# A conditioned block's second MLP: its first product divided a second time, into 49 inner products in seven streams

## The chip, the cores and the metric

The kernel runs on one core of one Trainium2 chip. The metric is the time of one execution on the device in microseconds (us). Before the change it is 484.83 us, the median of three executions that ran from 484.69 to 485.11 us. A separate execution was profiled; all rows of the profile come from that one.

## What is computed

Input `x` is 32 sequences of 128 tokens of 512 features, all float32. Two modulated MLPs follow one another. The first acts only on masked tokens (few of them). The second, which takes most of the time, acts on all 4096 tokens:

```
m = mask[:, :, None]
... # first half, on the masked tokens
x = x + gate_msa[:, None] * ssm_out
shift_mlp, scale_mlp, gate_mlp = jnp.split(silu(t) @ ffada_w + ffada_b, 3, axis=1)
ff_norm = _layernorm(x) * (1.0 + scale_mlp[:, None]) + shift_mlp[:, None]
h = gelu(ff_norm @ ff_w1 + ff_b1, approximate=True)      # 512 -> 1024
out = x + gate_mlp[:, None] * (h @ ff_w2 + ff_b2)        # 1024 -> 512
```

## The kernel before, in words

After an opening of about 93 us (masked tokens, weights, the first pair's normalised tokens) the second MLP runs over four pairs `p` of token groups. A pair is 8 sequences, 1024 tokens: side 0 and side 1, with 512 tokens each. Each of the two matrix products of a pair is done by a scheme of the Strassen-Winograd kind: tokens, features and outputs are halved, and seven inner products P1 to P7 of sums and differences of blocks take the place of eight.

*First product* (`first_product`, line 687). The sums of token blocks come from `combine_x` (L655 to L665: four VectorE subtractions and additions of 128x1024), those of the weights from `combine_weights` (L286, once). Output features are taken 128 at a time: four units `u`, two at a time ("U" and "V"), each with two PSUM banks `e` and `a` (`accumulators`, L671). `ORDER` (L582) gives the order of the 14 phases of two units, and a phase is one inner product of one unit: two matmul calls (L699) with a moving operand of 512 tokens. After P5, `keep_and_seed` (L676) copies `e` to SBUF and `a` into `e`, both on ScalarE. After P6, VectorE writes `e = a + P5` (L722). ScalarE applies GELU with its bias on the way out (L710). The hidden activations lie in `ha` (side 0) and `hb` (side 1).

*Second product* (`second_product`, line 733). The same 14 phases (called steps here) for two halves of the tokens: tokens are now the stationary operand, the moving one is a weight block of 256 columns, and a step is eight matmul calls (L756). `finish` (L772) multiplies the result by the gate and adds it to the `x` tile on VectorE, `store` (L782) sends the tile out on SP's queue. The output bias is added earlier: `add_bias` (L873) puts `gate * fb2` into the `x` tile, two VectorE operations for each of eight sequences.

*The next pair* is prepared under the matmuls by `fill`, lists of functions called after given steps. `load_x` (L297, SP's queue) and `take_first_half` (L562, eight indirect DMAs on GpSimd's queue) bring `x` in; `Statistics` (L584) computes mean and variance on VectorE and the root on GpSimd (L603); `blocks` normalises (L609) and transposes 32x32 squares (L909) on VectorE; `turned` (L631) moves the squares to their places with 16 DMAs per side on SP's queue; `scaled` (L640) modulates on ScalarE (L644); `combine_x` of the next pair is called after step 12. `gate_tiles` (L575) loads a pair's gates in one DMA on GpSimd's queue.

All five engines run in the order in which the program text issues their instructions (`manual_schedule`, L313): an instruction that waits holds back everything behind it on its engine. PSUM has three banks for `e` (`ps_h`, L91) and three for `a` (`ps_o`, L92).

## Time and profile before

| | |
|---|---|
| median of 3 executions | 484.83 us |
| profiled execution | 485.52 us, of which the page's span is 483.8 us |
| start of the first product of pair 0, and of pair 2 | 92.83 us, 285.65 us |
| end of the matmuls of pair 3 | 478.6 us (475.02 + 3.62) |
| VectorE busy | 278.3 us, 58% of the span |
| ScalarE busy | 132.6 us, 27% |
| GpSimd busy | 58.1 us, 12% |
| granted TensorE clock | 0.999 of full speed |

A profile row of a group names the line, the engine (PE is TensorE, PEld its weight loads, DVE VectorE, ACT ScalarE, POOL GpSimd, SP the queue of SyncE), the operation, output and inputs, the shapes and the count; then the busy time of the group in us, the mean of one in ns, and the idle time of the engine before them with what ended it. A float32 matmul call leaves two records, so a phase of two calls is four records. In the timeline a row has its start and its length in us.

### The profile page before, as it was taken

The numbers are of one execution on the slowest core, as the hardware profiler recorded it, in microseconds if no ns is written. First come the engines' busy times: TensorE is split into PE (matmuls) and PEld (weight loads), VectorE is DVE, ScalarE is ACT, GpSimd is POOL, SyncE is SP. The second block draws the span as 40 slices with busy tenths as digits, with TensorE's granted clock in tenths as the row PEclk, the third lists the DMA queues.
The fourth block names the chain that finished last, engine by engine and source line by source line (L and its number), as shares of the span: only waits on it lengthen the run. The fifth ranks groups of instructions, "written<-read, shape, count | busy, mean of one in ns | idle before, by whom it ended". The sixth has DMA issues, their size and how long they took to land.

```text
span 483.8 us, 4645 instructions
## 1 busy us (share of the span) xinstructions
PE 472.0 (98%) x1680; PEld 303.9 (63%) x1680; DVE 278.3 (58%) x458; ACT 132.6 (27%) x255; POOL 58.1 (12%) x75
## 2 busy tenths in 40 slices
PE   6899999999999999999999999999999999999995
PEld 2374484444458887444688874446888744468884
DVE  4623787937775647387746373876464734342645
ACT  3131024143322810332238002322371023221000
POOL 6210062017000000060000000600000000000000
PEclk9999999999999999999999999999999999999999
DMA  8999500091142312921323119113231160000012
GB/s 274 386 386 385 189 25 1 23 361 34 21 67 34 53 45 87 345 70 27 61 39 50 56 76 363 48 29 60 41 48 65 66 217 0 0 1 1 1 77 101
DMA packets 69995, 50.95 MB, mean 105 GB/s; under 512 B 54271, under 2 KB 54799, under 8 KB 69456
## 3 DMA queue, kind: packets, MB, share of 16 engines
q1 hardware_dynamic: 66240, 39.86, 27.2%
q0 software_dynamic: 3680, 10.75, 6.5%
q8 instruction: 15, 0.25, 0.2%
q14 instruction: 12, 0.10, 0.1%
q10 hardware_dynamic: 48, 0.00, 0.0%
HBM read 42.15 MB, written 9.50 MB: 107 GB/s over the span
## 4 chain that ended last, share of the span: by engine, by line
PE 94%; DVE 2%; issue 1%; POOL 1%; DMA 0%; DVEq 0%; POOLq 0%
PE a_h L699 23%; PE a_o L756 22%; PE e_o L756 17%; PE e_h L699 17%; PE ph_s L178 6%; PE po_s L192 5%; PE part_s L268 1%; PE pm_f L248 1%; PE last L756 1%; PE ptr L618 0%; DVE xT L623 0%; DMA mask_u<-in_mask_BxS_bk_dram 0%; PE ptr_s L169 0%; POOL xc L226 0%; PE pm_g L248 0%
## 5 line engine op out<-in xcount | busy, mean ns | idle before, releaser
L699 PE MATMUL e_h<-s,fw 128*128 128x512 f32 x128 | 60.1, 592 | 0.0
L756 PE MATMUL e_o<-fw,ha 128*128 128x256 f32 x256 | 57.9, 379 | 0.0
L699 PE MATMUL a_h<-xT,t 128*128 128x512 f32 x128 | 57.5, 592 | 0.0
L756 PE MATMUL a_o<-t,hb 128*128 128x256 f32 x240 | 53.1, 379 | 0.0
L756 PEld LDWEIGHTS e_o<-fw,ha 128*128 128x128 f32 x256 | 48.6, 190 | 6.6
L756 PEld LDWEIGHTS a_o<-t,hb 128*128 128x128 f32 x240 | 45.6, 190 | 6.2
L699 PEld LDWEIGHTS a_h<-xT,t 128*128 128x128 f32 x128 | 24.3, 190 | 30.6 <-issue 30.1
L699 PEld LDWEIGHTS e_h<-s,fw 128*128 128x128 f32 x128 | 24.3, 190 | 30.6 <-issue 29.9
L566 POOL DMA_INDIRECT x<-x_rows,slot_i x32 | 34.4, 1076 | 51.1 <-DMA x<-in_x_dram 32.1
L644 ACT ACTIVATE xT<-xT,modT 128x128 f32<-128x128 f32 x96 | 37.6, 481 | 6.7 <-DMA xT<-xn 6.7
L683 ACT COPY p_h<-e_h 128x512 f32<-128x512 f32 x16 | 9.4, 585 | 103.7 <-PE e_h L699 103.7
L722 DVE TENSOR_TENSOR e_h<-a_h,p_h 128x512 f32<-128x512 f32 x16 | 11.1, 695 | 45.3 <-PE a_h L699 45.2
L710 ACT ACTIVATE ha<-e_h,biasT 128x512 f32<-128x512 f32 x32 | 21.9, 685 | 48.2 <-PE e_h L699 48.2
L778 DVE TENSOR_TENSOR t_o<-e_o,gate 128x512 f32<-128x512 f32 x16 | 11.1, 691 | 35.9 <-PE e_o L756 35.9
L699 PE MATMUL a_h<-s,t 128*128 128x512 f32 x64 | 30.1, 592 | 0.0
L699 PE MATMUL e_h<-xT,fw 128*128 128x512 f32 x64 | 30.1, 592 | 0.0
L699 PE MATMUL a_h<-xT,fw 128*128 128x512 f32 x64 | 30.1, 592 | 0.0
L192 PE MATMUL po_s<-w,h_s 128*128 128x512 f32 x64 | 29.4, 594 | 0.0
L756 PE MATMUL e_o<-fw,s 128*128 128x256 f32 x128 | 28.9, 379 | 0.0
L756 PE MATMUL a_o<-fw,ha 128*128 128x256 f32 x128 | 28.9, 379 | 0.0
L756 PE MATMUL a_o<-t,s 128*128 128x256 f32 x128 | 28.9, 379 | 0.0
L178 PE MATMUL ph_s<-xT_s,w 128*128 128x256 f32 x128 | 28.7, 382 | 0.0
(149 smaller groups left out, 554.5 us busy)
## 6 DMA issues: line engine op xcount, KB each, us to landing
x<-in_x_dram SPq DMA_DIRECT2D x16, 512.0 KB, 11.0
gate<-gate_rows POOLq DMA_DIRECT2D x4, 2048.0 KB, 8.7
out_dram<-x SPq DMA_DIRECT2D x15, 512.0 KB, 2.8
xT<-xn SPq DMA_DIRECT2D x96, 64.0 KB, 2.3
fw<-in_L_cond_ff_w_dram SPq DMA_DIRECT2D x2, 2048.0 KB, 12.1
ada_f<-in_L_cond_ffada_w_dram SPq DMA_DIRECT2D x4, 768.0 KB, 10.1
ada_a<-in_L_cond_ada_w_dram SPq DMA_DIRECT2D x4, 512.0 KB, 5.7
w<-in_L_cond_ssm_w_dram SPq DMA_DIRECT2D x2, 1024.0 KB, 9.6
```

The lines of the kernel that those rows point to most:

```text
L178: nc.tensor.matmul(ph[:, :n], w[:, k, ts(f, P)], xT[:, k, :], start=(k == 0), stop=(k == KC - 1))
L192: nc.tensor.matmul(po, h[f][:, ts(i, P)], w[:, f, :], start=(f == 0), stop=(f == HC - 1))
L248: nc.tensor.matmul(pm[ts(j, B), :], sT[:, k, :], ada[:, k, ts(j, D)], start=(k == 0), stop=(k == KC - 1),)
L268: nc.tensor.matmul(t, picked[ts(j, B), ts(c, P)], mod[ts(j, B), :], start=True, stop=True)
L566: nc.gpsimd.indirect_dma_start(out=xs[i // G][i % G // 2][:, i % 2], out_offset=None, in_=x1_rows[:slots, :], in_offset=bass.IndirectOffse ...
L644: nc.scalar.activation(xT[:, k, ts(i, P)], xT[:, k, ts(i, P)], AF.Identity, bias=modT[:, k, b : b + 1], scale=modT[:, k, B + b : B + b + 1],)
L683: nc.scalar.copy(p5, e)
L699: nc.tensor.matmul(bank, w[product][:, k, ts(u, P)], xs[product][:, k, :], start=(product in ("P1", "P5") and k == 0), stop=True, skip_gro ...
L710: nc.scalar.activation(h[:, f, :], src, AF.Gelu_apprx_tanh, bias=biasT[:, 2 * KC + f : 2 * KC + f + 1],)
L722: nc.vector.tensor_tensor(e, a, p5[n], ALU.add)
L756: nc.tensor.matmul(part, src[:, k, ts(i, P)], w[product][:, k, :], start=(k == 0 if last else product in ("P1", "P5") and i == 0 and k == ...
L778: nc.vector.tensor_tensor(t, view, gate[:, g0 : g0 + 2, part], ALU.mult)
```

## The change

The first product is divided a second time. Each of the seven inner products of the outer scheme becomes a *stream* with an inner scheme of its own: 7 x 7 = 49 phases for a pair, in place of 28. A phase (`phase`) is again two matmul calls, now with a moving operand of 256 tokens. A stream has one bank `e` and one bank `a`, and yields a 2x2 set of blocks, named "11", "12", "21", "22". In the outer scheme a stream's result is either final (streams 2, 3 and 4, and 7 after an addition), and goes through GELU, or is kept in a quarter of `ha` and `hb` and added to a later stream's.

- Streams run in the order `STREAMS`. A `window` interleaves the last three phases of the old stream with the first four of the new one: new P5, new P1, old P3, old P7, new P2, new P6, old P4. There are six windows, called w1 to w6 here, between seven streams.
- The additions between streams: `seed` writes `e = a + earlier result` on VectorE (a ScalarE copy where there is none), `with_p5` and `after` add in SBUF on GpSimd: ten and eight a pair. P6, P7 and P4 of a stream end in a VectorE addition out of PSUM.
- Outer sums of tokens (`token_sums`, four sets of four VectorE operations a pair) and of weights (`weight_sums`, four sets of three, in pair 0 alone) are new. The sums of weights are stored to DRAM as `t_rows` and loaded again by `load_weights` in later pairs, on SP's queue, into the two buffers `g0` and `g1`, which the gates share; so the gates are loaded in two halves, during the second product.
- The output bias: `SecondProduct.seed` writes it into the accumulators (one ScalarE copy, one VectorE subtraction for each half of the tokens), and `add_bias` is gone. P1 and P5 of the second product no longer start afresh.
- The next pair is prepared at other places: `blocks` of side 1 after steps 3 and 4 of the second product (before: steps 0 and 1), `turned` of side 1 after step 4 and from the queues of SP and ScalarE in turn, the sums of `combine_x` one by one after steps 8 to 10, and the next pair's first stream (P5, P1, then P2, P6) between steps 11, 12 and 13. The last phases of stream 4 lie between steps 0, 1 and 2.

```diff
+    t_rows = dram.tile([4, P, 7, 2 * P], F32, name="t_rows")
...
-                nc.sync.dma_start(dst[ts(q, R), b], src[ts(b, R), q])
+                queues[b % len(queues)].dma_start(dst[ts(q, R), b], src[ts(b, R), q])
...
-    def first_product(p, xs, w, ha, hb, fillers):
...
+    STREAMS = (1, 2, 5, 6, 3, 7, 4)
+    PRIOR = {2: "21", 6: "21", 3: "12", 7: "21", 4: "21"}
+    RESULT = {1: "21", 2: "11", 5: "22", 6: "21", 3: "12", 7: "21", 4: "21"}
+    OF_X = {1: (0, 0), 2: (1, 0), 3: (1, 0), 4: (1, 1), 7: (0, 1)}
+    OF_W = {1: (0, 0), 2: (1, 0), 3: (1, 1)}
+    QT = 2 * P
...
+        def token_sums(self, j, n):
+            if (j, n) == (1, 0):
+                self.sx[5] = hp.tile([P, HC, QT], F32, tag="s1", name=f"sx_{self.p}")
+            if (j, n) == (2, 0):
+                t = group_of_tiles(f"sy_{self.p}")
+                self.sx[6] = t.rearrange("p g (h s) -> p (g h) s", s=QT)
+            add, sub = ALU.add, ALU.subtract
+            if j == 1:
+                s, a21, a22 = self.x.parts(n, self.sx[5], (0, 1), (1, 1))
+                nc.vector.tensor_tensor(s, a21, a22, add)
+            elif j == 2:
+                s1, a11 = self.x.parts(n, self.sx[5], (0, 0))
+                s2 = self.x.parts(n, self.sx[6])[0]
+                nc.vector.tensor_tensor(s2, s1, a11, sub)
+            elif j == 3:
+                _, a11, a21 = self.x.parts(n, self.sx[5], (0, 0), (0, 1))
+                nc.vector.tensor_tensor(a21, a11, a21, sub)
+            else:
+                s2, a12 = self.x.parts(n, self.sx[6], (1, 0))
+                nc.vector.tensor_tensor(a12, a12, s2, sub)
+        def weight_sums(self, j, n):
+            side = j % 2 == 0
+            if j < 3 and n == 0:
+                self.tw[side] = self.weight_tile(int(side))
+            b = {1: ((0, 1), (0, 0)), 2: ((1, 1),), 3: ((1, 1), (0, 1)), 4: ((1, 0),)}[j]
+            t, *b = self.w.parts(n, self.tw[side], *b)
+            if j % 2:
+                nc.vector.tensor_tensor(t, b[0], b[1], ALU.subtract)
+            else:
+                other = self.w.parts(n, self.tw[j == 4])[0]
+                nc.vector.tensor_tensor(t, b[0], other, ALU.subtract)
+            if n == len(self.w.views) - 1:
+                nc.sync.dma_start(t_rows[j - 1], self.tw[side][:, :7])
+        def load_weights(self, j):
+            side = j % 2 == 0
+            if j < 3:
+                self.tw[side] = self.weight_tile(int(side))
+            nc.sync.dma_start(self.tw[side][:, :7], t_rows[j - 1])
...
+        def phase(self, j, product):
+            if j not in self.banks:
+                self.banks[j] = accumulators(f"m{self.p}_{j}")
+                self.p5[j] = None
+            e, a = self.banks[j]
+            bank = bank_of(product, (e, a))
+            for n in range(2):
+                nc.tensor.matmul(
+                    bank[:, ts(n, QT)],
+                    self.w_block(j, product)[:, ts(n, P)],
+                    self.x_block(j, product),
+                    start=(product in ("P1", "P5") and n == 0),
+                    stop=True,
+                    skip_group_check=True,
+                )
+            e, a = (t.rearrange("p (n s) -> p n s", n=2) for t in (e, a))
+            prior, result = PRIOR.get(j), RESULT[j]
+            add = ALU.add
+            if product == "P5":
+                t = gp.tile([P, 512], F32, tag="p5", name=f"p5_m{self.p}_{j}", bufs=3)
+                self.p5[j] = p5 = t.rearrange("p (n s) -> p n s", n=2)
+                nc.scalar.copy(p5, e)
+                if prior and j not in (2, 4):
+                    self.with_p5(j, "12")
+                    self.with_p5(j, "22")
+            elif product == "P1":
+                if self.p5[j] is not None:
+                    self.seed(j)
+            elif product == "P2":
+                self.keep(j, "11", e)
+            elif product == "P6":
+                p5 = self.place(result, "12") if prior else self.p5[j]
+                nc.vector.tensor_tensor(e, a, p5, add)
+            elif product == "P3":
+                self.keep(j, "12", e)
+            elif product == "P7":
+                dst = self.place(result, "22")
+                nc.vector.tensor_tensor(dst, a, dst if prior else self.p5[j], add)
+                self.settle(j, "22")
+            elif product == "P4":
+                if prior:
+                    dst = self.place(result, "21")
+                    nc.vector.tensor_tensor(dst, a, self.place(prior, "21"), add)
+                    self.settle(j, "21")
+                else:
+                    self.keep(j, "21", a)
+        def seed(self, j):
+            e, a = (t.rearrange("p (n s) -> p n s", n=2) for t in self.banks[j])
+            if j in PRIOR:
+                nc.vector.tensor_tensor(e, a, self.place(PRIOR[j], "11"), ALU.add)
+            else:
+                nc.scalar.copy(e, a)
+        def with_p5(self, j, c):
+            other = self.place("22" if j == 3 else PRIOR[j], c)
+            nc.gpsimd.tensor_tensor(self.place(RESULT[j], c), self.p5[j], other, ALU.add)
+        def keep(self, j, c, src):
+            if j in (2, 3, 4):
+                self.gelu(RESULT[j], c, src)
+            else:
+                nc.scalar.copy(self.place(RESULT[j], c), src)
+                self.after(j, c)
+        def settle(self, j, c):
+            if j in (2, 3, 4):
+                self.gelu(RESULT[j], c, self.place(RESULT[j], c))
+            else:
+                self.after(j, c)
+        def after(self, j, c):
+            part = {q: self.place(q, c) for q in ("12", "21", "22")}
+            if j == 6:
+                other = part["12"] if c in ("12", "22") else part["22"]
+                nc.gpsimd.tensor_tensor(part["12"], part["21"], other, ALU.add)
+            elif j == 7:
+                nc.gpsimd.tensor_tensor(part["22"], part["21"], part["22"], ALU.add)
+                self.gelu("22", c, part["22"])
+        def window(self, new, old, fill):
+            for n, (j, product) in enumerate(
+                (
+                    (new, "P5"), (new, "P1"), (old, "P3"), (old, "P7"),
+                    (new, "P2"), (new, "P6"), (old, "P4"),
+                )
+            ):
+                self.phase(j, product)
+                if new in (2, 4) and n in (2, 3):
+                    self.with_p5(new, "12" if n == 2 else "22")
+                for f in fill.get(n, ()):
+                    f()
...
+        def seed(self, c):
+            self.banks[c] = e, a = accumulators(f"o{self.p}_{c}")
+            e, a = (t.rearrange("p (i d) -> p i d", i=2) for t in (e, a))
+            b0, b1 = (
+                fb2[:, ts(h, D // 2)].unsqueeze(1).to_broadcast([P, 2, D // 2]) for h in range(2)
+            )
+            nc.scalar.copy(a, b0)
+            nc.vector.tensor_tensor(e, b1, b0, ALU.subtract)
...
-        def add_bias(i):
-            t = tp.tile([P, D], F32, tag="t", name=f"t_b{p}_{i}")
-            nc.vector.tensor_tensor(t, gate[:, i], fb2, ALU.mult)
-            xt = xs[i // G][i % G // 2][:, i % 2]
-            nc.vector.tensor_tensor(xt, xt, t, ALU.add)
...
-        first_product(p, xs1, fw1_of, ha, hb, fill)
...
-            put(0, blocks, 1, (0, 1))
-            put(1, blocks, 1, (2, 3))
-            put(2, to_feature_rows, 1)
-            for k in range(KC):
-                put(4 + k, lambda k: scaled(2 * (p + 1), xT[0], k), k)
-                put(8 + k, lambda k: scaled(2 * (p + 1) + 1, xT[1], k), k)
...
+    now = FirstProduct(0, of_x[0].cut(), of_w)
+    for j in (1, 2):
+        now.do(j, "P1")
+    for n in range(3):
+        now.weight_sums(1, n)
+    for n in range(4):
+        now.token_sums(1, n)
+    now.do(1, "P5")
+    now.seed(1)
+    now.do(2, "P5")
+    now.do(1, "P2", "P6", "P3")
+    now.seed(2)
+    now.with_p5(2, "12")
+    now.do(1, "P7")
+    now.with_p5(2, "22")
+    now.do(2, "P2")
+    for n in range(2):
+        now.token_sums(2, n)
+    now.do(2, "P6")
+    for n in range(2, 4):
+        now.token_sums(2, n)
+    now.do(1, "P4")
+    now.weight_sums(2, 0)
...
+        if p == 0:
+            put(2, 1, now.weight_sums, 2, 1)
+            put(2, 3, now.weight_sums, 2, 2)
+            for n, at in enumerate((1, 3, 4)):
+                put(4, at, now.weight_sums, 3, n)
+                put(5, at, now.weight_sums, 4, n)
+        else:
+            put(3, 6, now.load_weights, 3)
+            put(4, 6, now.load_weights, 4)
+            for n, at in enumerate((3, 4, 6, 6)):
+                put(1, at, now.token_sums, 2, n)
+        for n, at in enumerate((3, 4, 6, 6)):
+            put(2, at, now.token_sums, 3, n)
+        for n, at in enumerate((1, 3, 4, 6)):
+            put(3, at, now.token_sums, 4, n)
+        put(6, 3, second.seed, 0)
+        put(6, 3, second.first_block, 0, 0, 2)
+        put(6, 6, second.first_block, 0, 2, 4)
+            if p == 0:
+                x_of[1] = load_x(1)
...
+            put(1 if p else 2, 6, take_first_half, p + 1, x_next, range(G))
+            put(2, 6, take_first_half, p + 1, x_next, range(G, 2 * G))
+            put(3, 6, stats[0].one, 0)
+            put(4, 3, stats[0].one, 1)
+            put(4, 6, stats[0].one, 2)
+            put(5, 3, stats[0].one, 3)
+            put(5, 3, stats[0].root)
+            put(5, 4, blocks, 0, 0)
+            put(5, 6, blocks, 0, 1)
+            put(6, 4, blocks, 0, 2)
+        for w in range(1 + (p == 0), 7):
+            now.window(STREAMS[w], STREAMS[w - 1], fills.get(w, {}))
+        second.load_gate(0)
+        second.step(0)
+        second.seed(1)
+        now.do(4, "P3", "P7")
+        if more_pairs:
+            blocks(0, 3)
+            to_feature_rows(0, nc.sync)
+            stats[1].one(0)
+        second.step(1)
+        now.do(4, "P4")
+        second.load_gate(1)
+        for lo in (0, 2):
+            second.first_block(1, lo, lo + 2)
...
+            for i in range(1, G):
+                put(2, stats[1].one, i)
+            put(2, stats[1].root)
+            for i in range(G):
+                put(3 + i // 2, blocks, 1, i)
+            put(4, to_feature_rows, 1, nc.sync, nc.scalar)
+            for k in range(KC):
+                put(4 + k // 2, lambda k: scaled(2 * (p + 1), xT[0], k), k)
+                put(7 + k // 2, lambda k: scaled(2 * (p + 1) + 1, xT[1], k), k)
...
+            put(8, begin, 1)
+            put(9, begin, 2)
+            put(9, begin, 3)
+            put(10, begin, 4)
+            def next_product():
+                nxt["p"] = FirstProduct(p + 1, of_x[p + 1].cut(), of_w)
+                nxt["p"].load_weights(1)
+            put(10, next_product)
+            put(11, lambda: nxt["p"].do(1, "P5", "P1"))
+            for n in range(4):
+                put(11 + n // 2, lambda n: nxt["p"].token_sums(1, n), n)
+            if p + 2 < NP:
+                x_of[p + 2] = [[], []]
+                put(11, lambda: x_of[p + 2][0].extend(load_side(p + 2, 0)))
+                put(13, lambda: x_of[p + 2][1].extend(load_side(p + 2, 1)))
+            put(12, lambda: nxt["p"].do(1, "P2", "P6"))
+            put(13, lambda: nxt["p"].load_weights(2))
+        for step in range(2, len(ORDER)):
+            second.step(step)
+            for f in fill.get(step, ()):
+                f()
+        if more_pairs:
+            now = nxt["p"]
```

## The prediction, made before the changed kernel was run

> **What bounds the kernel now.** I read the page's busy shares and its chain of waits first, then the timeline of TensorE in both products.
>
> ```profile
> PE 472.0 (98%) x1680; PEld 303.9 (63%) x1680; DVE 278.3 (58%) x458; ACT 132.6 (27%) x255; POOL 58.1 (12%) x75
> ...
> PE 94%; DVE 2%; issue 1%; POOL 1%; DMA 0%; DVEq 0%; POOLq 0%
> ```
>
> TensorE is busy throughout and 94% of the chain is its own work. Whether that is work or waiting shows in the rhythm of phases:
>
> ```profile
> 116.86 1.88 PE L699 MATMUL a_h<-xT,fw 128*128 128x512 f32 x4
> 118.58 1.88 PE L699 MATMUL e_h<-s,fw 128*128 128x512 f32 x4
> ```
>
> ```profile
> 244.21 3.62 PE L756 MATMUL a_o<-fw,ha 128*128 128x256 f32 x16
> 244.41 0.59 ACT L683 COPY p_o<-e_o 128x512 f32<-128x512 f32 x1 [6.22 <-PE e_o L756]
> ...
> 254.57 3.62 PE L756 MATMUL a_o<-t,s 128*128 128x256 f32 x16
> ```
>
> A first-product phase (4 records, 512 columns) starts every 1.717 us, a second-product step (16 records, 256 columns) every 3.454 us (244.21 to 254.57 is three steps). 14 x 2 x 1.717 = 48.1 and 14 x 3.454 = 48.4 make 96.4 a pair, and pair 0 to pair 2 took 192.8 = 2 x 96.4: between phases TensorE never waits. So fewer columns pay in full, and any new wait costs in full. A reader on another engine starts 0.20 after a phase's nominal end (244.41 against 244.21).
>
> The prices of the other engines, from the groups by shape and the timeline:
>
> ```profile
> L780 DVE TENSOR_TENSOR x<-x,t_o 128x512 f32<-128x512 f32 x32 | 22.1, 692 | 1.1
> L597 DVE BATCH_NORM_STATS2 st<-x 128x6 f32<-128x512 f32 x32 | 21.8, 681 | 0.8 <-DMA x<-x_rows,slot_i 0.8
> L609 DVE TENSOR_SCALAR xn<-x,mv,rstd 128x512 f32<-128x512 f32 x32 | 16.3, 525 | 3.3 <-POOL rstd L603 3.3
> L683 ACT COPY p_h<-e_h 128x512 f32<-128x512 f32 x16 | 9.4, 585 | 103.7 <-PE e_h L699 103.7
> L603 POOL TENSOR_TENSOR rstd<-ve,half 128x4 f32<-128x4 f32 x8 | 8.7, 1082 | 51.4 <-DVE ve L602 51.4
> L182 ACT ACTIVATE h_s<-ph_s,biasT 128x256 f32<-128x256 f32 x16 | 7.6, 473 | 21.3 <-PE ph_s L178 21.3
> L351 POOL IOTA slot_row<- 128x512 f32 x1 | 0.6, 557 | 0.0
> masks.py:199 POOL TENSOR_SCALAR_AFFINE_SELECT ident<-ident 128x128 f32<-128x128 f32 x1 | 0.3, 291 | 0.1
> masks.py:197 POOL MEMSET ident<- 128x128 f32 x1 | 0.2, 204 | 0.3 <-POOLq L1049 0.3
> ```
>
> ```profile
> 248.16 10.70 SPq L638 DMA_DIRECT2D xT<-xn  x16
> ...
> 252.42 6.26 ACT L644 ACTIVATE xT<-xT,modT 128x128 f32<-128x128 f32 x16
> ```
>
> ```profile
> 300.88 1.07 POOL L566 DMA_INDIRECT x<-x_rows,slot_i  x1 [10.88 <-DMA x<-in_x_dram]
> 302.26 1.01 POOL L566 DMA_INDIRECT x<-x_rows,slot_i  x1 [0.31 <-issue]
> ```
>
> Back to back, a VectorE addition of 128x512 comes every 0.66, a statistic with its aggregate every 0.82, normalising plus transposing every 1.2, 128x1024 every 1.17. Gathers come every 1.31.
>
> **The gain.** A new phase is 4 records of 256 columns: 3.454 / 4 = 0.863. 49 x 0.863 = 42.3 against 48.1: 5.75 a pair, **23.0 in all**. Weight loads stay hidden (190 ns against 216 a record, as in L756).
>
> **What costs nothing.** `add_bias` (16 VectorE operations a pair, 10.6 us) goes, and VectorE was not on the chain; its work is replaced by 16 token sums (about 10) and, a pair, some 16 more additions out of PSUM (11). They hide under TensorE where VectorE keeps up; a window lasts 7 x 0.863 = 6.04 and holds 4 additions (2.6) plus 2.4 to 4 of fillings. Where it doesn't, I count it below. Gates in halves are due 20 us after they are asked for, against 8.7 us to landing for the whole before. The stores of weight sums only occupy SP's queue (fourth wait).
>
> **The unknown price** is a 128x512 addition on GpSimd, call it *t*: 18 a pair. Below, the 128x512 iota, which reads nothing: 0.557. Above, four 128x128 selects, twice for two inputs: 2.33. In between, each 512-column input costs 4 x (0.291 - 0.204) = 0.35 over a pure write, so 0.557 + 2 x 0.35 = **1.25**, which I take; the nearest two-input row, the power of 128x4, is 1.08.
>
> [...]
>
> **The waits that I find**, each followed by hand through the order of instructions on its engine:
>
> 1. *Start of pair 0, once: 3.6.* VectorE ends the opening's last addition at 96.15. Ahead of the first P6 addition stand three weight sums (0.66 + 0.66 + 0.95) and four token sums (2.4): the addition ends at 101.5, P3 of stream 1 can start at 101.6. TensorE would be there at 92.83 + 6 x 0.863 = 98.0.
> 2. *End of every first product, 2.7 x 4 = 10.8.* In w6, ScalarE's copy that seeds `a` of the second product stands behind two GELUs of stream 7's "22", and these behind GpSimd. From the window's start: stream 7's P3 ends at 2.6, ScalarE copies it (3.4), GpSimd does `after` "12", `with_p5` of stream 4, `after` "22" (3 x 1.25: 7.15), two GELUs of 128x256 (2 x 0.47: 8.1), the copy (8.7). Step 0 could start at 6.04. The other queues behind it don't matter: TensorE stands still.
> 3. *w5 and w6, pairs 0 to 2: 7.0.* `root` and the first `blocks` now stand in front of stream 7's P6 addition: P7 addition to 4.3, statistics 5.3, GpSimd's power 6.4, block 7.6, addition 8.3; P3 is due at 7.77: 0.6. Then P4 addition, second block and the seed of stream 4 end at 10.85, where P2 is due at 10.1: 0.8. So 1.4 x 3; pair 0 has three weight sums more in w5 (2.3) and in w4 (0.5).
> 4. *Gathers of pair 0: 1.2.* `load_x` now stands behind the first store of weight sums (98.4 in place of 96.55); eight gathers (10.5) run to some 117 to 119, then GpSimd makes three additions before the seed of stream 3 can start: 120.7 to 122.7. With wait 1, w4 starts at 118.0, P2 of stream 3 is due 4 x 0.863 later, its seed (0.66) by 120.8: a wait of 0 to 2.5; I take the middle.
> 5. *Into the next pair, 1.3 x 3 = 3.9.* `blocks` of side 1 end 25.05 after step 0's start (step 4's matmuls end at 19.86, then `finish` 1.34, a subtraction 1.15, two blocks 2.4). ScalarE issues eight DMAs (0.63 each, half of the 10.7 row being 16 x 0.67: 5.0) and scales both sides (2 x 6.26): 42.6. VectorE's first sum of `begin` waits for that, with everything of steps 9 to 13 behind it. Added up: the addition that frees step 13's bank ends at 51.25 (due 50.9), stream 1's P6 addition and the seed of stream 2 come 0.6 and 0.3 late.
> 6. *Loading the second weight sums, pairs 1 and 2: 2.0 x 2 = 4.0.* `load_weights(2)` stands on SP's queue behind two loads of `x` that wait for the stores of step 13; I get its issue 7.0 after w1's start. Stream 6 needs it at 12.1. At the 386 GB/s of the page's best slice, 1.4 MB take 3.7 plus some 1.4: no wait. With the 11.0 to landing of the `x` loads: a wait of 5. Gathers run at the same time, so I take 2.
>
> Sum: 3.6 + 10.8 + 7.0 + 1.2 + 3.9 + 4.0 = 30.5, less 23.0: **+7.5**. On the profiled execution's 485.52 that is 493.0; the median stands 0.69 lower, so **492.3**. *t* enters about 15 times (wait 2 twelve times, wait 4 three times).
>
> **The rivals.**
>
> *A: the GpSimd additions are cheap, and it is faster.* One place, wait 2 (and 4), one price, *t*. At the iota's 0.557 the sum falls by 15 x 0.69 = 10.4: 481.9. It decides from *t* = 0.75 (7.5 / 15 below 1.25). For it: GpSimd is idle 88% of the time, and memset and select rows are short. Against: no row with two long inputs.
>
> *B: GpSimd becomes the bound of the first product.* A pair needs 18 x *t* + 8 x 1.31 + 2 x 1.08 = 12.6 + 18 *t* there, and all of it falls into the windows, 6 x 6.04 = 36.2: full from *t* = 1.31. At 2.33 my sum alone gives 492.3 + 16.2 = 508.5; more where additions queue. For it: 35.1 of 36.2 even at 1.25. Against: the waits themselves stretch the windows.
>
> [...] Before, gathers beside VectorE go from 1.0 to 1.3 or 1.4 us now and then, and VectorE's rows don't stretch. [...]
>
> *C: the smaller phases don't run at 0.863.* Then the gain is gone: 484.8 + 30.5 = 515. Against it: L756 has the same shapes at 216 ns a record.
>
> **How the numbers follow.** My forecast (487 to 500) 0.48; A 0.25; B 0.20; C 0.03; waits and gain even out 0.04. Measurements of this kernel tell a change from none at about 0.2%, 1 us. So faster 0.25, same 0.04, slower 0.71. The range goes from a cheap addition with loads in time (481.9 - 3) to B's 508.5 with a little queueing: 479 to 510.
>
> **What will show it.** Four records every 0.863 in the first product, or C. GpSimd's additions at 1.25, below 0.75 (A) or near 2 (B). TensorE idle before step 0 in each of four pairs, released by ScalarE's copy, by 2 to 4 us: wait 2. VectorE waiting at GpSimd's power in w5 (3); at ScalarE's scaling before the first sum of `begin` (5); TensorE waiting for the weight-sum DMA at stream 6 (6). If TensorE shows no idle time over 1 us at these places, my sum is wrong.

## The result, and the profile after

| | before | after |
|---|---|---|
| median in the same comparison | 484.97 us | 521.08 us (4 executions, 516.60 to 524.19) |
| profiled execution | 485.52 us | 520.54 us, span 518.8 us |
| ratio to before | | 1.0736, 95% interval 1.0656 to 1.0817 |

The changed kernel is slower, as forecast, but by 36 us and not by 7.5: the time lies outside the range of 479 to 510. The ratios leave out executions over 1.5% above a kernel's fastest; where they scatter (e3, e9), the text gives the times.

First the page of the changed kernel: busy time of each engine, the granted TensorE clock in 40 slices, and the shares of the chain of waits.

```profile
PE 469.5 (90%) x2016; PEld 374.5 (72%) x2016; DVE 362.2 (70%) x542; ACT 171.7 (33%) x371; POOL 160.4 (31%) x151
...
PEclk9999999998979999989999989998899999989999
...
PE 43%; DVE 25%; ACT 10%; issue 7%; DMA 7%; POOL 6%; ACTq 2%; SPq 0%; DVEq 0%; POOLq 0%
```

TensorE's own share of the chain fell from 94% to 43%, VectorE's rose from 2% to 25%. VectorE is busy 84 us more than before, where the parts of the prediction (10 + 11 - 10.6 a pair) give some 42. And the clock row has 7s and 8s, which the row of before hadn't.

The phases themselves are as forecast: in TensorE's timeline (start, busy time, line, tiles, records) a new one starts every 0.86 us.

```profile
107.99 1.03 PE L840 MATMUL a_m<-xT,t 128*128 128x256 f32 x4
108.85 1.03 PE L840 MATMUL e_m<-sx,tw 128*128 128x256 f32 x4
...
118.83 1.03 PE L840 MATMUL a_m<-xT,fw 128*128 128x256 f32 x4
124.55 2.02 PE L840 MATMUL e_m<-xn_sy,tw 128*128 128x256 f32 x4 [4.70 <-DVE e_m L865]
126.36 1.87 PE L840 MATMUL a_m<-xn_sy,tw 128*128 128x256 f32 x4
128.07 1.03 PE L840 MATMUL e_m<-xT,fw 128*128 128x256 f32 x4
```

At 118.83 in w4 of pair 0 the next phase starts 5.72 us later, 4.86 more than 0.863, and the two phases after the wait take 1.81 and 1.71 in place of 0.863. Taking every start-to-start distance this way (0.863 a phase, 3.454 a step, distances over the wait put down as waiting, the rest as half clock) gives, for all four pairs:

| place | predicted | waiting | half clock behind it |
|---|---|---|---|
| wait 1, start of pair 0 | 3.6 | 3.1 | 0 |
| wait 2, before step 0 | 10.8 | 11.2 | 5.0 |
| wait 3, w5 and w6 | 7.0 | 11.2 | 2.7 |
| wait 4, w3 and w4 (pairs 0, 2, 3) | 1.2 | 9.3 | 1.8 |
| wait 5, into the next pair | 3.9 | 7.3 | 1.5 |
| wait 6, second weight sums | 4.0 | 4.1 | 1.8 |
| sum | 30.5 | 46.2 | 12.8 |

59.0 less the gain of 23.0 is 36.0; the two profiled executions differ by 35.0, so the table is right to 1 us. Three waits had the right size in sum, three were too small by 15.7 together, and 12.8 us of half clock were not in the prediction's sum at all.

What held w4 in pair 0? VectorE's timeline, then GpSimd's, at that place:

```profile
115.73 0.68 DVE L870 TENSOR_TENSOR hb<-a_m,p_m 128x512 f32<-128x512 f32 x1
116.33 7.56 DVE L774 TENSOR_TENSOR xT<-xT,xn_sy 128x512 f32<-128x512 f32 x2
123.81 0.69 DVE L865 TENSOR_TENSOR e_m<-a_m,ha 128x512 f32<-128x512 f32 x1
```

```profile
116.17 1.01 POOL L576 DMA_INDIRECT x<-x_rows,slot_i  x1 [0.30 <-issue]
117.19 1.29 POOL L891 TENSOR_TENSOR ha<-p_m,ha 128x512 f32<-128x512 f32 x1
118.42 1.27 POOL L891 TENSOR_TENSOR hb<-p_m,hb 128x512 f32<-128x512 f32 x1
119.65 1.26 POOL L913 TENSOR_TENSOR ha<-ha 128x512 f32<-128x512 f32 x1
120.86 1.25 POOL L891 TENSOR_TENSOR ha<-p_m,ha 128x512 f32<-128x512 f32 x1
122.08 1.25 POOL L891 TENSOR_TENSOR hb<-p_m,hb 128x512 f32<-128x512 f32 x1
```

Two token sums, which take 1.28 us together where they run alone (in e8 and e12 below), took 7.56, and ended half a microsecond after GpSimd's fifth addition in a row. The row of VectorE holds two instructions: the first took 0.68 us, the second, from 116.93 on, 6.96. GpSimd came straight from a gather (L576) into the five additions. The P6 addition that TensorE waits for (L865) is itself 0.69, but stood behind them. The groups by line of the changed kernel show which VectorE instructions are stretched (the last two figures before the bar: busy us in all and mean ns of one):

```profile
L620 DVE TENSOR_SCALAR xn<-x,mv,rstd 128x512 f32<-128x512 f32 x32 | 22.2, 711 | 5.6 <-POOL rstd L614 5.6
L774 DVE TENSOR_TENSOR xT<-xT,xn_sy 128x512 f32<-128x512 f32 x8 | 17.1, 2171 | 0.0
L959 DVE TENSOR_TENSOR s<-hb 128x512 f32<-128x512 f32 x16 | 14.9, 952 | 3.9 <-ACT hb L815 3.9
L865 DVE TENSOR_TENSOR e_m<-a_m,ha 128x512 f32<-128x512 f32 x20 | 13.7, 687 | 9.7 <-ACT ha L815 7.9 <-ACT ha L898 1.5 <-POOL ha L913 0.4
L954 DVE TENSOR_TENSOR e_o<-fb 128x512 f32<-128x512 f32 x8 | 12.0, 1503 | 0.0
```

Sums of two SBUF operands (L774, L959, L954) and the normalising (L620) are long; an addition with one operand in PSUM (L865) stays at 687 ns.

The clock, in the view of equal stretches (stretch, length, busy us and instructions of PE, PEld, DVE, ACT, POOL, granted clock, DMA):

```profile
121.19:124.60 3.41, 0.05 (x1) 0.05 (x1) 3.41 (x3) 0.00 (x0) 2.14 (x2) 1.00 0.00 0
124.60:128.01 3.41, 3.41 (x8) 2.76 (x9) 2.23 (x5) 0.58 (x1) 0.67 (x1) 0.51 0.01 2
...
250.90:254.31 3.41, 1.61 (x8) 1.08 (x6) 3.41 (x3) 0.97 (x3) 3.33 (x3) 1.00 0.00 0
254.31:257.73 3.42, 2.21 (x10) 1.98 (x11) 2.14 (x5) 1.92 (x5) 1.19 (x2) 1.00 0.00 0
356.73:360.14 3.41, 1.07 (x5) 0.59 (x4) 3.38 (x3) 0.97 (x3) 3.33 (x3) 1.00 0.00 0
360.14:366.97 6.83, 6.16 (x15) 4.91 (x16) 3.79 (x5) 2.77 (x7) 2.82 (x3) 0.50 0.07 29
```

A stretch of 3.41 us in which TensorE was busy for 0.05 us is followed by one at half clock (0.51). The wait of 3.01 us before step 0 of pair 1 leaves it busy for 1.61 and 2.21 us in two stretches, and the clock stays at 1.00; the wait of 3.01 us in pair 2 leaves 1.07 us in one, and 6.83 us at 0.50 follow. In all, the trace has six stretches at half clock between the first phase and the last step, from 124.60, 141.67, 223.58, 302.11, 360.14 and 462.53 on, each 3.41 or 6.83 us long; the starts lie whole multiples of 3.413 us apart, and the stretches of the view lie on the same points.

### The profile page after: what moved, and what is told of

Its sections match the earlier page's. It is cut to its first block, busy times and chain, and to the rows that moved or that the text cites. A ratio compares the mean times of both kernels' runs of the same rounds, so it can differ in the third digit from the quotient of the medians.

```text
span 518.8 us, 5805 instructions
## 1 busy us (share of the span) xinstructions
PE 469.5 (90%) x2016; PEld 374.5 (72%) x2016; DVE 362.2 (70%) x542; ACT 171.7 (33%) x371; POOL 160.4 (31%) x151
## 4 chain that ended last, share of the span: by engine, by line
PE 43%; DVE 25%; ACT 10%; issue 7%; DMA 7%; POOL 6%; ACTq 2%; SPq 0%; DVEq 0%; POOLq 0%
PE a_o L1005 10%; PE e_o L1005 8%; PE a_m L840 7%; ACT xT L655 6%; PE e_m L840 6%; PE ph_s L184 5%; PE po_s L198 3%; DMA tw<-t_rows 3%; DVE xn L620 2%; DVE t_o L979 2%; DVE s L685 2%; ACTq L649 2%; DVE x L981 2%; DMA xT<-xn 2%; DVE sx L764 2%
## 5 line engine op out<-in xcount | busy, mean ns | idle before, releaser
L891 POOL TENSOR_TENSOR ha<-p_m,ha 128x512 f32<-128x512 f32 x20 | 26.4, 1319 | 165.4 <-ACT ha L898 154.4
L815 ACT ACTIVATE hb<-hb,biasT 128x256 f32<-128x256 f32 x64 | 29.0, 500 | 44.7 <-POOL hb L915 22.3
L1005 PE MATMUL a_o<-fw,ha 128*128 128x256 f32 x128 | 34.1, 427 | 10.4 <-ACT a_o L953 10.4
L576 POOL DMA_INDIRECT x<-x_rows,slot_i x32 | 35.2, 1101 | 19.6 <-DMA x_rows<-t_s 10.6
L1005 PEld LDWEIGHTS a_o<-fw,ha 128*128 128x128 f32 x128 | 27.4, 217 | 16.4 <-ACT a_o L953 12.0
L898 ACT COPY ha<-e_m 128x512 f32<-128x512 f32 x32 | 18.5, 579 | 41.8 <-PE e_m L840 36.3
L840 PE MATMUL e_m<-s,fw 128*128 128x256 f32 x96 | 25.7, 393 | 6.5 <-DVE s L685 4.2
L854 ACT COPY p_m<-e_m 128x512 f32<-128x512 f32 x28 | 16.3, 581 | 43.1 <-PE e_m L840 43.1
L891 POOL TENSOR_TENSOR hb<-p_m,hb 128x512 f32<-128x512 f32 x20 | 29.1, 1457 | 0.3
L184 PEld LDWEIGHTS ph_s<-xT_s,w 128*128 128x128 f32 x128 | 24.0, 190 | 4.6 <-ACT h_s L188 1.5
L1005 PEld LDWEIGHTS a_o<-t,s 128*128 128x128 f32 x128 | 24.4, 190 | 3.3
L1005 PEld LDWEIGHTS e_o<-fw,s 128*128 128x128 f32 x128 | 24.4, 190 | 3.2
```

What stands on the lines that cost most here:

```text
L184: nc.tensor.matmul(ph[:, :n], w[:, k, ts(f, P)], xT[:, k, :], start=(k == 0), stop=(k == KC - 1))
L576: nc.gpsimd.indirect_dma_start(out=xs[i // G][i % G // 2][:, i % 2], out_offset=None, in_=x1_rows[:slots, :], in_offset=bass.IndirectOffse ...
L815: nc.scalar.activation(dst[:, n], src[:, n], AF.Gelu_apprx_tanh, bias=biasT[:, f : f + 1])
L840: nc.tensor.matmul(bank[:, ts(n, QT)], self.w_block(j, product)[:, ts(n, P)], self.x_block(j, product), start=(product in ("P1", "P5") and ...
L854: nc.scalar.copy(p5, e)
L891: nc.gpsimd.tensor_tensor(self.place(RESULT[j], c), self.p5[j], other, ALU.add)
```

## The experiments

My theory: VectorE's sums of two SBUF operands and GpSimd's additions lengthen each other, as in the rows above (a sum of 0.68 us took 6.96; I call this exclusion); order on VectorE, ScalarE and SP, and half clock behind waits. The rival throughout: only the order of instructions counts, the rest is off the path. All ratios are to the kernel before, run beside each experiment (485.13 to 485.42 us).

### e1: ScalarE's copy ahead of the GELUs

`seed_a` is the part of `seed` that holds the copy, `nc.scalar.copy(a, b0)`.

```diff
...
+        put(6, 1, second.seed_a, 0)
         put(6, 3, second.seed, 0)
```

> ScalarE's copy that seeds a of the second product is emitted in w6 right after P1 of stream 4, ahead of the GELUs that wait for GpSimd; nothing else moves. Theory (wait 2 is the order on ScalarE, and the half clock in two of the four steps 0 comes from it): step 0 loses its waits of 1.6, 3.3, 3.3 and 3.3 us, about 0.9 of each comes back one stop later, when P3 of stream 4 waits for its P6 addition; with the half clock that follows, 8 to 13 us less than the changed kernel: 508 to 513, and no ScalarE copy among the releasers of step 0. Rival (another instruction is ready no sooner, the wait only changes its name): 517 or more, with step 0 or the phase behind it idle for the same 3 us.

508.70 us (507.92 to 509.72), ratio 1.0482 (1.0465 to 1.0500): within what was expected. The prediction's second wait is what it was said to be. In the changed kernel, before step 0 of pair 1, on TensorE and on ScalarE:

```profile
255.52 3.72 PE L1005 MATMUL a_o<-fw,ha 128*128 128x256 f32 x16 [3.01 <-ACT a_o L953]
```

```profile
254.08 0.91 ACT L815 ACTIVATE hb<-hb,biasT 128x256 f32<-128x256 f32 x2 [2.44 <-POOL hb L915]
254.90 0.57 ACT L953 COPY a_o<-fb 128x512 f32<-128x512 f32 x1
```

The copy stands behind GELUs that wait 2.44 us for GpSimd. With the copy early, step 0 no longer waits; 1.1 us (0.9 expected) come back at P3 of stream 4 in pairs 1 to 3.

### e2: all additions on VectorE

```diff
-            nc.gpsimd.tensor_tensor(self.place(RESULT[j], c), self.p5[j], other, ALU.add)
+            nc.vector.tensor_tensor(self.place(RESULT[j], c), self.p5[j], other, ALU.add)
...
-                nc.gpsimd.tensor_tensor(part["12"], part["21"], other, ALU.add)
+                nc.vector.tensor_tensor(part["12"], part["21"], other, ALU.add)
...
-                nc.gpsimd.tensor_tensor(part["22"], part["21"], part["22"], ALU.add)
+                nc.vector.tensor_tensor(part["22"], part["21"], part["22"], ALU.add)
```

> All 18 additions a pair that GpSimd makes between streams go to VectorE, at the same places of the program. Theory (GpSimd and VectorE exclude each other where VectorE has two SBUF inputs): the rows stretched beside GpSimd return to their length alone, L774 from 2171 to about 690 ns, L959 from 952 to 690, L620 from 711 to 530; the two long waits behind the token sums of w3 and w4 go, and ScalarE's GELUs no longer wait for GpSimd; VectorE gets 18 x 0.6 = 10.9 us a pair more, of 42.3: 492 to 510. Rival (the waits come from the number of instructions ahead in VectorE's order, the exclusion is a side matter): 10.9 us a pair more on an engine whose windows w3 to w6 are full, 525 to 540.

500.44 us (499.69 to 502.29), ratio 1.0304 (1.0287 to 1.0321): 20.6 us less, with 72 instructions more on VectorE. The groups by line of e2:

```profile
L620 DVE TENSOR_SCALAR xn<-x,mv,rstd 128x512 f32<-128x512 f32 x32 | 16.6, 533 | 2.6 <-POOL rstd L614 2.3
L959 DVE TENSOR_TENSOR s<-hb 128x512 f32<-128x512 f32 x16 | 10.6, 686 | 3.9 <-ACT hb L815 3.9
L954 DVE TENSOR_TENSOR e_o<-fb 128x512 f32<-128x512 f32 x8 | 5.5, 693 | 0.0
L774 DVE TENSOR_TENSOR xT<-xT,xn_sy 128x512 f32<-128x512 f32 x8 | 5.5, 682 | 0.0
```

Same instructions, same operands; only GpSimd's additions are gone, and each row is back at its length alone. These four rows lost 28.0 us of busy time (5.6 + 4.3 + 6.5 + 11.6). The rival's 525 to 540 is refuted. But e2 shows what the additions on GpSimd cost, not what the exclusion costs by itself: counted by place as above, the profiled executions of the changed kernel and of e2 lose 59.1 and 41.3 us, and 10.6 of these 17.8 lie at step 0 and behind it (16.2 against 5.6), where ScalarE waits for GpSimd's additions and the prediction had a wait without any exclusion.

### e3: the token sums of w3 earlier

```diff
-        for n, at in enumerate((1, 3, 4, 6)):
+        for n, at in enumerate((0, 0, 1, 2)):
             put(3, at, now.token_sums, 4, n)
```

> The four token sums for stream 3 move from places 1, 3, 4, 6 of w3 to 0, 0, 1, 2, so that they are made before GpSimd starts its additions there. Same instructions, same engines. Theory (exclusion): the pair of sums that took 7.56 us in pair 0 and 5.38 in pair 2 takes 1.3, the waits at the start of w4 in pair 0 (4.9, and 1.8 by the half clock behind it) and in pair 2 (3.2) go: 510 to 514. Rival (VectorE is late there because of what it has to do in all, so the order inside w3 doesn't matter, or the sums are now in the way of the seed of stream 6): 518 to 526, with the idle time at the start of w3 or w4.

514.99 us (511.13, 514.39, 515.59, 522.80), ratio 1.0563 (1.0524 to 1.0602). The median lies between the two ranges. In pair 2 the wait (3.2 us) is gone; in pair 0 one sum still ran into GpSimd's additions, took 4.75 us, and TensorE waited 3.6 us three phases earlier than before, at the end of w3. The mean of L774 fell to 1250 ns, not to 690.

### e4 and e5: matmuls in the waits

The numbers shown are those of e5 (in e4 they are 6 and 12); further calls stand ahead of the other waits.

```diff
...
+    def keep_busy(n):
+        t = ps_t.tile([P, 512], F32, tag="tr", name="busy")
+        row = of_w.raw("P1", 0, 0)
+        for _ in range(n):
+            nc.tensor.matmul(
+                t[:, :QT], row[:, :P], row, start=True, stop=True, skip_group_check=True
+            )
...
+        keep_busy(3 if p == 0 else 6)
         second.step(0)
```

> Matmuls on constant operands into an unused PSUM bank stand ahead of the waits of the changed kernel, each group shorter than the wait: 16 records (3.5 us) in pair 0 before P3 in w4 and w6, 6 (1.3) before step 0 of pair 0, 6 in pairs 1 and 2 at the starts of w3 and before P3 in w6, 12 (2.6) before step 0 of pairs 1 to 3, 6 before the first phase of the next pair. They add work to TensorE and remove no wait. Theory (some 13 us of the changed kernel are phases at half the clock behind a wait): the profile shows granted clock above 0.99 and the time is 506 to 512 though TensorE has 24 us more of matmuls. Rival (the low clock comes with something else than TensorE's own pause, or costs nothing because the phases behind a wait are not on the path): 518 or more; if the records delay what they precede, up to 540.

524.29 us (523.04 to 530.75), ratio 1.0845 (1.0775 to 1.0915), no stretch of half clock. The time is in the rival's range (518 or more), but my count was wrong (two records a call), and with 50 us of matmuls added it doesn't tell the two apart.

> The kernel of e4 with half as many calls: in e4 each call became two records (232 in all, 50.1 us of TensorE work, where I had counted 25), so the groups were longer than the waits. Now 116 records, 25 us. Theory (phases behind a wait run at half the clock, some 13 us in all): granted clock above 0.995, 506 to 512 though TensorE does 25 us more. Rival (the half clock costs nothing in the end, because what it delays waits anyway): 518 to 524 at the same clock.

516.15 us (513.93 to 521.07), ratio 1.0663 (1.0597 to 1.0730). Granted clock 0.999, no half stretch, against six stretches (27.3 us, so 13.7 us lost by the clock's own record) in the changed kernel. So with TensorE busier in the waits the clock stayed up: from 121.19 to 124.60, where the changed kernel had it busy for 0.05 us, it was busy for 2.16. That it also paid is not shown: the medians differ by 4.9 us and the profiled executions by 5.8, but the intervals of the two ratios overlap (1.0597 to 1.0730, 1.0656 to 1.0817). The time lies between the two expectations. The inserted records stand in program order and also delay phases that were ready.

### e6: loads and scaling reordered

```diff
-            put(4, to_feature_rows, 1, nc.sync, nc.scalar)
             for k in range(KC):
-                put(4 + k // 2, lambda k: scaled(2 * (p + 1), xT[0], k), k)
+                put(3, lambda k: scaled(2 * (p + 1), xT[0], k), k)
+            put(4, to_feature_rows, 1, nc.sync, nc.scalar)
...
+            put(13, lambda: nxt["p"].load_weights(2))
                 put(13, lambda: x_of[p + 2][1].extend(load_side(p + 2, 1)))
-            put(13, lambda: nxt["p"].load_weights(2))
```

> Two steps of the preparation are moved, at places of the trace that can be read apart: the loading of the second weight sums stands ahead of the loads of x on SP's queue (wait 6), and ScalarE scales side 0 in step 3, before it issues its half of side 1's DMAs (wait 5). Theory (the order on these two queues): TensorE's waits for tw<-t_rows (2.5 and 1.3, with 1.8 of half clock) go, and the first sum of the next pair no longer waits 9.5 us for ScalarE's scaling but some 3, so TensorE's waits for it (1.3, 1.9, 1.0, with 1.5 of half clock) go: 508 to 514. Rival (the gate tile that the weight sums overwrite, and VectorE's finishing of steps 9 to 13, set both): 517 or more, the waits with the same length under another releaser.

518.12 us (517.41 to 521.31), ratio 1.0671 (1.0653 to 1.0689): a miss. Both waits did go (no wait for the weight sums is left; the starts of pairs 1 to 3 lose about 1 us together). But now TensorE reached w3 and w4 earlier in pairs 1 and 2, and there the sums met the additions, as in pair 0. VectorE of e6:

```profile
225.29 7.55 DVE L774 TENSOR_TENSOR xT<-xT,xn_sy 128x512 f32<-128x512 f32 x2
```

Waits of 4.8 and 5.3 us with half clock behind them took the gain back.

### e7: preparation of side 0 out of w5 and w6

```diff
...
-            put(5, 3, stats[0].root)
-            put(5, 4, blocks, 0, 0)
-            put(5, 6, blocks, 0, 1)
-            put(6, 4, blocks, 0, 2)
...
+            put(5, 0, stats[0].root)
+            put(5, 6, blocks, 0, 0)
+            put(6, 6, blocks, 0, 1)
...
+            blocks(0, 2)
             blocks(0, 3)
```

> Statistics of side 0 stand one place earlier in w4, the root goes to the first place of w5, and the four blocks to the last places of w5 and w6 and behind step 0. Theory (wait 3: VectorE's P6 addition for stream 7 stands behind the root on GpSimd and a block stretched by GpSimd's additions): the waits before P3 in w6 (4.0 in pair 0 with 2.7 of half clock, 1.7 in pairs 1 and 2) and before P2 there (0.9) go, wait 2 stays: 506 to 514. Rival (GpSimd's backlog delays the additions of w6 anyway): 516 or more, with VectorE or ScalarE waiting at POOL's additions in the same places.

515.72 us (511.22 to 517.49), ratio 1.0595 (1.0544 to 1.0647): between the two expectations. The waits of 4.0 and 1.7 us before P3 in w6 are gone, so their place was right. But step 0 of pair 0 now waits 3.2 us with 3.0 of half clock behind it (1.5 and none before), and w4 of pairs 1 and 2 waits 3.0 and 4.6 (none and 3.0 before).

### e8: all of it together

In addition to e1, e6 and e7: the first sums of `s1` behind step 0, the token sums of pair 0 behind stream 2's seed, and this choice of engine:

```diff
-            nc.gpsimd.tensor_tensor(self.place(RESULT[j], c), self.p5[j], other, ALU.add)
+            adder = nc.gpsimd if j in (3, 7) else nc.vector
+            adder.tensor_tensor(self.place(RESULT[j], c), self.p5[j], other, ALU.add)
...
-                nc.gpsimd.tensor_tensor(part["22"], part["21"], part["22"], ALU.add)
+                nc.vector.tensor_tensor(part["22"], part["21"], part["22"], ALU.add)
```

> All steps together: ScalarE's copy early (e1), the order of weight loads and scaling (e6), the preparation of e7, the first sums of s1 behind step 0, the token sums of pair 0 behind stream 2's seed, and on VectorE those of GpSimd's additions that stand beside VectorE instructions with two SBUF inputs (with_p5 of streams 2, 6, 4, and stream 7's own), the other ten stay. Theory (waits 1 to 6, exclusion and half clock make up the 58 us of lost time, and each can be taken away): some 10 to 20 us of waits are left, no stretch of half clock over 3.4 us: 468 to 484, faster than before. Rival (VectorE with 5 us more a pair becomes the bound of w3 and w6): 487 to 500.

482.84 us (482.63 to 484.16), ratio 0.9953 (0.9939 to 0.9968): faster than both kernels, by 2.6 us (0.5%) against before, and within what was expected. Of the 18 additions a pair, ten moved to VectorE and eight stay on GpSimd (the expectation says ten stay). Its page:

```profile
PE 456.8 (95%) x2016; PEld 364.5 (76%) x2016; DVE 354.7 (74%) x578; ACT 171.7 (36%) x371; POOL 108.3 (23%) x111
...
PEclk9999999999999999999999999999999999999999
```

No stretch of half clock. About 22 of the 59 us of lost time are left, in waits of up to 1.5 us.

### e9, e12: the remaining waits

e9 moves stream 6's `with_p5` behind its seed, GELUs one phase later, and work out of w6. e12 is e8 with the token sums of w3 earlier, stream 6's `with_p5` behind its seed, one block and stream 4's second `with_p5` behind step 0, and the statistics one place later:

```diff
...
-        for n, at in enumerate((1, 3, 4, 6)):
+        for n, at in enumerate((0, 1, 1, 2)):
             put(3, at, now.token_sums, 4, n)
...
+                part = {(2, 2): "12", (2, 3): "22", (6, 3): "12", (6, 5): "22", (4, 2): "12"}
```

> The kernel of e8 with four changes, each for a wait that its trace still shows: with_p5 of stream 6 behind the seed of stream 6 (1.0 us at the start of P2 in w3, four times), GELUs of settled quarters one phase later on ScalarE, behind the copy that the next seed needs (0.45), stream 4's second with_p5 and the blocks of side 0 out of w6 (0.5 and 0.6), and in pair 0 the blocks behind step 0, because w4 and w5 hold six weight sums there. Theory (what is left are waits of order on VectorE and ScalarE, each worth its length): 2.5 us a pair and some 2 of pair 0: 470 to 478. Rival (VectorE is full in w3 and w6, a moved instruction only moves the wait): 480 to 485.

Ten executions from 484.47 to 499.45 us, median 492.95; ratio 1.0032 (0.9991 to 1.0073), no difference from before that is clear of noise. The fastest of the ten is slower than the slowest of e8: a miss. The profile is of the execution of 499.45 us. VectorE and GpSimd of e9 in pair 1:

```profile
221.65 5.71 DVE L775 TENSOR_TENSOR s<-s,xn_sy 128x256 f32<-128x256 f32 x1
```

```profile
221.12 1.01 POOL L576 DMA_INDIRECT x<-x_rows,slot_i  x1 [0.30 <-issue]
222.15 1.27 POOL L926 TENSOR_TENSOR ha<-ha 128x512 f32<-128x512 f32 x1
...
225.81 1.25 POOL L926 TENSOR_TENSOR ha<-ha 128x512 f32<-128x512 f32 x1
```

One sum of 256 columns, 0.41 us where it runs alone, came half a microsecond before GpSimd's four additions, while a gather ran, and ended after them. TensorE waited 4.4 to 4.8 us for it in three pairs.

> The kernel of e8 (additions of streams 3 and 7 and of the result of 6 on GpSimd, the rest on VectorE) with three changes: the four token sums for stream 3 at places 0, 1, 1, 2 of w3, so that the last of them ends some 2 us before GpSimd's first addition there (in e9 a sum of 0.41 us that came 0.5 us too late took 5.71); stream 6's with_p5 behind its seed; stream 4's second with_p5 and one block more behind step 0. Theory (a sum is held for as long as GpSimd's additions follow each other, so where the sums end before them nothing is held; the waits of 1.0 at w3, 0.5 and 0.6 in w6 of e8 go): L774 and the 256-column sum at 690 and 410 ns in all pairs, clock 1.0, 474 to 480. Rival (VectorE's total in w3 and w6 sets the time, as e11's 486 suggests, and moved work returns as another wait): 482 to 488.

483.58 us (482.61 to 490.30), ratio 0.9959 (0.9944 to 0.9974). The sums are at their own length in all pairs, as VectorE's timeline in pair 1 shows, and the clock is 1.0:

```profile
213.99 0.42 DVE L774 TENSOR_TENSOR s<-s,xn_sy 128x256 f32<-128x256 f32 x1
```

So the half of the expectation on the sums holds, though the exclusion isn't gone: stream 6's second `with_p5` (L892), now on VectorE beside GpSimd's first addition, takes 2.00 us in place of 0.68. The time is the rival's: the wait of 1.0 us in w3 is gone (0.4 in w4 in its place), but the one before step 1 grew from 0.6 to 1.2, and those of 0.5 in w6 stayed.

### e10, e11: one pair of kernels that differs in the engine alone

e9's text with all 18 additions a pair on GpSimd (e10) or on VectorE (e11); no other line differs between the two.

> The kernel of e9 with all 18 additions a pair on GpSimd, as in the changed kernel; every other step stays as in e9. Theory (the exclusion costs by itself, because VectorE's token sums and first sums are held while GpSimd's additions follow each other): L774 above 1000 ns, waits at w3 and w4 back; 8 to 20 us more than e9, 482 to 498. Rival (it only cost because other work was late too): within 3 us of e9, with VectorE's rows as long but nothing waiting for them.

> The kernel of e9 with all 18 additions a pair on VectorE: no exclusion at all, but 8 additions a pair (5 us) more than e9, in w4 and w5 and for stream 6's sums. Theory (only additions beside VectorE's two-input instructions are dear on GpSimd, and VectorE has 42 us a pair of which e9 leaves little in w4 and w5): 2 to 10 us more than e9. Rival (any addition on GpSimd costs more than on VectorE): the same as e9 or less.

e10: 515.92 us (515.70 to 516.82), ratio 1.0632 (1.0613 to 1.0652). e11: 485.95 us (484.67 to 486.82), ratio 1.0013 (1.0001 to 1.0025). 30 us between them, with 34.1 us of half-clock stretches in e10 and 3.4 in e11: the additions are dear on GpSimd even where everything else has been put in order. Here the exclusion can be placed. Of the four token sums of stream 3, the one of 256 columns, first in e10, then in e11:

```profile
L775 DVE TENSOR_TENSOR s<-s,xn_sy 128x256 f32<-128x256 f32 x4 | 17.6, 4404 | 0.0
```

```profile
L775 DVE TENSOR_TENSOR s<-s,xn_sy 128x256 f32<-128x256 f32 x4 | 1.6, 411 | 0.0
```

In e10 it took 5.73 us in pairs 1 and 2 and 5.74 in pair 0. 18 of the 30 us lie in w4, where TensorE waits behind it, waits and half clock together (22.7 us lost there in e10, 4.4 in e11). e10 is slower than its own range of 482 to 498. e11 was expected 2 to 10 us above e9; by the ratios (1.0013 and 1.0032, with overlapping intervals) the two can't be told apart, so that was wrong. e8, with eight additions a pair left on GpSimd, is 3.1 us faster than e11, though the two differ in more than that.

## Why the prediction was right or wrong

- *Gain 23.0*: right. Rival C is out.
- *GpSimd's addition at 1.25*: right; 47 of the 72 took 1.25 to 1.29 us. The others, each beside a VectorE sum of two SBUF operands or the normalising, took 1.33 to 1.81. Rival A is out.
- *Wait 1*, 3.6: measured 3.1. *Wait 2*, 10.8: measured 11.2, released by the copy as said; e1 confirms the cause. Its size is in part luck: 2.7 in each pair was forecast, and it is 3.3 in pairs 1 to 3 and 1.6 in pair 0, where w6 had already lost 4.0 us. *Wait 6*, 4.0: measured 4.1 (2.7 and 1.5); e6 confirms the cause, but the size was chosen between 0 and 5 a pair, so that it fits is luck.
- *Wait 3*, 7.0: right place (e7), measured 11.2: 4.6 in pair 0, 2.8 in pairs 1 and 2, where 1.4 each was forecast, and 0.8 in pair 3. In pairs 1 and 2 the power on GpSimd took 1.04 us, as counted, but the normalising behind it ran beside one of GpSimd's additions and took 1.50 in place of 0.53; in pair 0 both were stretched (1.69 and 1.49).
- *Wait 5*, 3.9: right cause (e6), measured 7.3. No row of VectorE is stretched here. `blocks` end 25.1 us after step 0's start in pairs 0 and 1, as forecast, and the scaling takes 12.4, as forecast; the term that was mis-sized is ScalarE's issuing of eight DMAs, 5.0 in the sum and 6.5, 7.1 and 6.3 us in pairs 0, 1 and 2:

```profile
280.69 7.11 ACTq L649 DMA_DIRECT2D xT<-xn  x8
287.98 12.42 ACT L655 ACTIVATE xT<-xT,modT 128x128 f32<-128x128 f32 x32 [14.56 <-DMA xT<-xn]
```

- *Wait 4*, 1.2: the gathers were right, the mechanism was not. I had a seed waiting for GpSimd's additions; what waited was VectorE, inside a token sum, and in pairs 2 and 3 too. Measured 9.3.
- *The step that failed* is how the sum priced VectorE and TensorE: VectorE's instructions "back to back" by the rows of before, where no addition ran on GpSimd, and every phase at 0.863. The sum has no term for what VectorE and GpSimd cost each other, and none for the clock. In their place the runs showed VectorE busy for 42 us more than its parts give, 12.3 us missing in waits 3 and 4, and 12.8 us of half clock; the DMA issues of wait 5 make the other 3.4. Together this is the error to 1 us.

Of the order between the two engines the traces show this: the sum of 0.68 us that took 6.96 started 0.26 us ahead of GpSimd's five additions and ended half a microsecond after the fifth; the sum of e9 started 0.5 us ahead and ended 0.3 us after the fourth. A gather was running on GpSimd both times.

For the clock, the trace of the changed kernel shows this much: in the 3.41 us before its six half-clock stretches TensorE was busy for 0.05, 1.10, 0.93, 1.53, 1.07 and 0.83 us, and after two spans with 1.61 us (from 97.29 and from 250.90) the clock stayed at 1.00.

Left open: how much of waits 3 and 4 is exclusion and how much plain order, and what holds a sum for a whole row. Taking the additions off GpSimd is worth 20.6 us in the changed kernel (e2), but that also takes away half clock, the longer additions and the waits for GpSimd. And an obvious rival was not tried: wherever the timelines of both engines in the changed kernel, e3, e4, e6 and e9 show token sums held for more than 3 us (to 6.96 and 3.67 us in pairs 0 and 2 of the changed kernel, to 4.75 in e3, to 3.07 in e4, two sums to 7.55 together in e6, to 5.71 in e9), the row of additions began 0.01 to 0.03 us after the end of a gather on GpSimd. In pair 3, where no gathers run, the same sums of the changed kernel were held for one addition each (1.1 to 1.8 us). Gathers moved elsewhere might have ended the long holds with the additions where they are; no run shows it.

## What to carry to other kernels

Before work goes to an idle engine, list what the neighbours run beside it: 72 additions, priced at their own length and hidden but for waits 2 and 4, cost 20 to 30 us more on GpSimd than on VectorE (e2; e10 against e11). A wait on TensorE can be priced twice, once for itself and once for the clock behind it: 46.2 us of waits had 12.8 us of half clock behind them here. And where several waits lie in a row, taking one away brings the next forward into the same conflict (e6, e7): they have to be taken away together (e8).

## What the runs showed of the hardware

- Sums were held for three to five GpSimd additions in a row (4.75, 5.71 and 6.96 us), also when the sum was the first to start, 0.5 us ahead (a gather was then running on GpSimd). At most other places the two engines alternated, also where one addition followed the other without a pause: in w6 of the changed kernel 1.14 to 1.77 us a VectorE instruction on SBUF operands, 1.25 to 1.71 an addition; in e12 a VectorE instruction beside two such additions was held for the first alone (2.00 us). What decides between the two is open.
- Normalising, with one operand of 512 columns in SBUF, was held as well (1.50 us against 0.53); additions with one operand in PSUM were not (L865 687 ns in the mean).
- The same wait didn't always cost clock: the 3.01 us before step 0 of the changed kernel had full clock behind them in pair 1 and 6.83 us at half clock in pair 2. In e9 the time goes with the clock that was granted (484.47 us at 0.993, 499.45 at 0.979). But half clock doesn't have to scatter the times (e10: 0.966 to 0.973, four executions within 1.1 us), and they scatter with little of it too (e5: 0.993 to 0.999, 7.1 us apart).
